# A four-layer linear-attention encoder stage: its engine order written out by hand, its attention placed between the other half's feed products

## The chip, the cores and the metric

The kernel runs on one core of a Trainium2 chip. The metric is device microseconds of one execution of the whole kernel, in which the stage spoken of here is one of eleven.

## The reference, cut to what matters

The kernel computes a four-layer network on 16 sequences of 64 tokens with 256 features (1024 tokens). The second stage of layer 0, `l0_attn` in the kernel, is an encoder of its own with four layers, all in float32:

```python
def _linear_attention(q, k, v):
    qp = jax.nn.elu(q) + 1.0
    kp = jax.nn.elu(k) + 1.0
    kv = jnp.einsum('bshd,bshm->bhmd', kp, v)
    ksum = jnp.sum(kp, axis=1)
    z = 1.0 / (jnp.einsum('blhd,bhd->blh', qp, ksum) + EPS_ATTN)
    return jnp.einsum('blhd,bhmd,blh->blhm', qp, kv, z)

def _encoder_layer(x, ...):
    h = _layernorm(x, ln1_s, ln1_b)
    q, k, v = h @ Wq + bq, h @ Wk + bk, h @ Wv + bv      # 16 heads of 16
    x = x + (_linear_attention(q, k, v) @ Wo + bo)
    h = _layernorm(x, ln2_s, ln2_b)
    return x + (relu(h @ W1 + b1) @ W2 + b2)             # 256 -> 1024 -> 256
```

The stage is `x = x + LN(encoder(sqrt(256) * LN(x) + pos))`: the encoder works on a copy `y`, and the last LayerNorm (`lnf_s`, `lnf_b`) is added to the residual x. A later stage, a cross attention over a context of 16 x 1601 rows, needs the sum of squares of each context row; these sums have nothing to do with the encoder, but they are taken during this stage, 208 instructions of 128 rows each.

## The kernel before

The 1024 tokens are eight tiles of 128, in two halves of four tiles, `a` and `b` (class `Half`). Each half goes through three steps per layer:

- `project`: `norm` (statistics, a square root on ScalarE, the normalisation), transposes to feature-major `hT`, the queries `qT` by feature (`by_feature`, 512 columns a product), keys `kz` and values `va` by token (`by_token`), then `elu1` (lines 338 to 340) over the whole half: a minimum with 0 on GpSimd, Exp on ScalarE, and a combination on VectorE, once for the queries and once for the keys.
- `attend`: per tile of 128 tokens (two sequences j) the key-value sums `pk` (`sums`, line 493: 64 rows of the array), masked on VectorE to `kv`; then `apply` (line 504: 64 columns of the array) to `po`; division on VectorE, transposes, the output product with `wo` and its addition to `y` (line 526).
- `feed`: `norm` and transposes again, W1 by feature with ReLU (`bias_relu`, lines 345 and 347, alternating VectorE and ScalarE), W2 by token.

`add_row` (line 429) adds an output bias to the whole half of `y` on GpSimd. `squares(n)` draws the next n of the context's sums of squares (`context_squares`, lines 2059 to 2070) and is called after each product; their input comes in 32 pieces over SyncE's DMA queue, and with this calling pattern all 208 are done in the first 150 us of the stage.

The order of the work is the scheduler's. The program text gives priorities (for each layer: project a, feed b of the layer before, attend a, project b, feed a, attend b), and the scheduler places every instruction on its engine by its own estimate of when its inputs are there. An engine works off its queue strictly in that order. Other stages of the kernel have their TensorE instructions in written order instead: with `self.pinned` set, `mm` and `tr` call `keep_in_program_order` on each instruction. [...]the stage uses two each for `mm`, `tr`, `kv` and `po`.

## Time and profile before

| | |
|---|---|
| median of three runs | 3892.77 us (3888.97 to 3895.52) |
| the profiled execution's own time | 3895.43 us |
| its span, first to last instruction | 3893.4 us |
| granted TensorE clock, mean | 0.958 of full |
| the stage: last product of the stage before ends, last `x` of this one is written | 864.8 to 1363.6 us |
| busy in 860 to 1365: TensorE, VectorE, ScalarE, GpSimd | 438.3, 257.9, 162.1, 101.5 us |

The profile is that of one execution. A row of the timeline has the start in us, the length in us, the engine, the line of the kernel, the operation, output<-input, its shape and how many are merged in the row; in brackets is how long the engine stood idle before it and what released it. PE is TensorE (PEld its weight loads), DVE VectorE, ACT ScalarE, POOL GpSimd, SPq the queue of SyncE that issues DMAs. A float32 product appears as two MATMUL records. In the table of windows each row is one stretch of time: its bounds, its length, then the busy time of each engine with the number of its instructions in brackets, the granted TensorE clock (1.00 is full), the DMA share and GB/s. A period of the steady state, one half through one layer, takes 58.4 us: the same transposes begin at 1146.2, 1204.6 and 1263 us.

### The profile page before, as it was taken

How to read it: one execution, taken by the hardware profiler on the slowest of the kernel's cores; microseconds unless marked ns; L12 is line 12 of the kernel's file. 1: busy time of each engine (PE TensorE's matmuls, PEld its weight loads, DVE VectorE, ACT ScalarE, POOL GpSimd, SP SyncE). 2: the span in 40 equal slices, each digit the busy share in tenths (PEclk: the TensorE clock that was granted, in tenths of full speed). 3: DMA queues.
4: the chain of work that ended last, by engine and by line, in shares of the span. 5: the costliest groups of instructions: out<-in, count | busy, mean ns of one | idle time of the engine just before them, and what ended most of it. 6: DMA issues, size and time to landing. Idle time of an engine off the chain costs nothing.

```text
span 3893.4 us, 71039 instructions
## 1 busy us (share of the span) xinstructions
PE 3559.3 (91%) x31163; PEld 2254.0 (58%) x31178; DVE 2001.7 (51%) x3655; ACT 1415.8 (36%) x1987; POOL 1311.5 (34%) x756
## 2 busy tenths in 40 slices
PE   8999999988989889999987898899999889999985
PEld 4555555555556555555545666567777656555554
DVE  4334333345454445655656554567676656333346
ACT  2333333346411111444433433266666612111223
POOL 1555555552221101433431100377777630000011
PEclk9999999999999989999998999999999979999987
DMA  3111111015200005222401000311111004111640
GB/s 122 37 37 37 37 37 37 19 52 204 101 33 25 22 22 176 106 77 100 141 26 38 1 6 1 104 40 54 37 55 37 2 10 167 39 35 32 286 156 13
DMA packets 97373, 248.84 MB, mean 64 GB/s; under 512 B 7924, under 2 KB 68991, under 8 KB 94888
## 3 DMA queue, kind: packets, MB, share of 16 engines
q1 hardware_dynamic: 97064, 244.31, 17.7%
q8 instruction: 244, 4.00, 0.4%
q14 instruction: 65, 0.53, 0.0%
HBM read 243.24 MB, written 1.05 MB: 63 GB/s over the span
## 4 chain that ended last, share of the span: by engine, by line
PE 55%; DVE 10%; ACT 3%; issue 2%; POOL 1%; DMA 1%; DVEq 0%; ACTq 0%; SPq 0%; POOLq 0%
PE pk L2050 9%; PE sc L2050 7%; PE lin L179 5%; PE pu L2050 3%; PE acc L2050 3%; PE gate L1622 3%; PE up L1622 3%; PE pc L1249 3%; PE prz L2050 2%; PE lin_t L166 2%; PE lin L445 2%; PE turn L2055 1%; PE gelu_t L1159 1%; PE lin_t L435 1%; PE lin L2050 1%
## 5 line engine op out<-in xcount | busy, mean ns | idle before, releaser
L1986 POOL TENSOR_TENSOR tot<-tot,e 128x1024 f32<-128x1024 f32 (+1 forms) x340 | 803.0, 2362 | 375.0 <-ACT e L307 252.2
L250 DVE TENSOR_REDUCE m<-sc 128x4 f32<-128x2048 f32 x96 | 220.1, 2293 | 273.3 <-PE sc L2050 272.2
L1389 DVE SCALAR_TENSOR_TENSOR e<-sc,row_L_xattn_nbias,free 128x2048 f32<-128x2048 f32 x104 | 244.3, 2349 | 124.5 <-PE sc L2050 118.9
L1391 ACT ACTIVATE e<-e 128x2048 f32<-128x2048 f32 x104 | 198.7, 1910 | 243.3 <-DVE e L1389 243.3
L2050 PE MATMUL sc<-qb,kT 32*128 32x128 f32 x6656 | 247.2, 285 | 39.6 <-DVE m L264 12.3
L307 ACT ACTIVATE e<-sc 128x2048 f32<-128x2048 f32 x104 | 195.2, 1877 | 241.5 <-PE sc L2050 236.5
L2050 PEld LDWEIGHTS sc<-qb,kT 32*128 32x128 f32 x6656 | 208.2, 188 | 84.8 <-issue 25.1
L2050 PE MATMUL acc<-e,v 128*32 128x128 f32 x6656 | 228.4, 278 | 6.7 <-ACT e L1392 6.6
L2050 PEld LDWEIGHTS acc<-e,v 128*32 128x32 f32 x6656 | 171.4, 110 | 105.4 <-issue 95.0
L2050 PE MATMUL pk<-cT,wk 128*128 128x512 f32 (+1 forms) x512 | 207.6, 534 | 3.6 <-DVE rows L280 3.6
L2050 PE MATMUL pk<-wv,cT 128*128 128x256 f32 x832 | 208.6, 393 | 0.0
L1392 ACT ACTIVATE e<-e 128x2048 f32<-128x2048 f32 x104 | 198.7, 1911 | 3.3
L2050 PE MATMUL pk<-cT,wkv 128*128 128x512 f32 (+1 forms) x512 | 196.5, 524 | 0.0
L2050 PE MATMUL pk<-wkv,cT 128*128 128x256 f32 x832 | 196.3, 386 | 0.0
L2050 PEld LDWEIGHTS pk<-wv,cT 128*128 128x128 f32 x832 | 149.2, 189 | 75.3 <-issue 57.2
L2050 PEld LDWEIGHTS pk<-wkv,cT 128*128 128x128 f32 x832 | 153.2, 190 | 28.4 <-issue 4.3
L1249 PE MATMUL pc<-ew,eh 128*128 128x256 f32 x640 | 159.0, 392 | 0.0
L794 POOL TENSOR_TENSOR e<-e,mx 128x512 f32<-128x512 f32 x96 | 81.6, 882 | 211.9 <-DVE mx L793 211.9
L2050 PE MATMUL sc<-kT,qb 32*128 32x512 f32 (+2 forms) x1536 | 140.3, 462 | 13.0 <-issue 1.5
L2050 PE MATMUL pu<-cn,e 128*64 128x257 f32 (+1 forms) x1248 | 143.9, 387 | 5.6 <-POOL e L804 5.6
L1626 ACT ACTIVATE g<-gate 128x512 f32<-128x512 f32 x68 | 40.6, 597 | 293.3 <-PE gate L1622 293.3
L2050 PE MATMUL sc<-cT,qT 128*64 128x512 f32 (+1 forms) x768 | 142.3, 519 | 1.0 <-DVE qT L752 0.5
(484 smaller groups left out, 6434.2 us busy)
## 6 DMA issues: line engine op xcount, KB each, us to landing
cT<-in_ctx_t SPq DMA_DIRECT2D x128, 832.0 KB
cn<-in_ctx_n SPq DMA_DIRECT2D x32, 1664.0 KB
piece<-in_ctx_n SPq DMA_DIRECT2D x16, 896.0 KB
piece<-in_ctx_n SPq DMA_DIRECT2D x16, 768.0 KB
w<-in_L_attn_W SPq DMA_DIRECT2D x8, 1024.0 KB
w<-in_L_ffn_W SPq DMA_DIRECT2D x16, 256.0 KB
down<-in_L_ffn_w_down SPq DMA_DIRECT2D x16, 256.0 KB
gate<-in_L_ffn_w_gate SPq DMA_DIRECT2D x16, 256.0 KB
```

The costliest lines, as they stand in the source:

```text
L166: nc.tensor.matmul(pm, w[:, k, n * P : (n + 1) * P], xT[:, k, h * 512 : (h + 1) * 512], start=(k == 0), stop=(k == kc - 1),)
L179: nc.tensor.matmul(pm, xT[:, k, t * P : (t + 1) * P], w[:, k, :], start=(k == 0), stop=(k == kc - 1))
L250: nc.vector.tensor_reduce(x.m4[:, g, :, i], pm, AX.X, ALU.max)
L307: nc.scalar.activation(e, pm, AF.Exp, scale=0.25)
L794: pin(nc.gpsimd.tensor_tensor(p.e, p.e, p.mx.unsqueeze(2).to_broadcast(p.shape), ALU.subtract))
L1249: nc.tensor.matmul(pc[:, n, j, :], s.eh[i][:, c, tok], ew2[:, c, cols], start=False, stop=(c == 3))
L1389: nc.vector.scalar_tensor_tensor(e16, pm16, nb, free[:, at : at + P].unsqueeze(1).to_broadcast([P, 16, P]), ALU.add, ALU.mult)
L1391: nc.scalar.activation(e, e, AF.Relu)
L1392: nc.scalar.activation(e, e, AF.Square)
L1622: nc.tensor.matmul(pm[-1], w[:, k, n * P : (n + 1) * P], xT[:, k, tok], start=(k == 0), stop=(k == KC - 1))
L1986: nc.gpsimd.tensor_tensor(tot[:w], x.first if c == 1 else tot[:w], e[:w], ALU.add)
L2050: ins = self.nc.tensor.matmul(*args, **kw)
```

## The change

`Written` wraps an engine so that each of its instructions is kept in program order. In `l0_attn` all of VectorE's, ScalarE's and GpSimd's instructions go through it (`V`, `A`, `G`), and TensorE's through `mm` and `tr` with `pinned` set. The steps become generators that stop after each piece, and hand-written loops step them: `project` of one half alongside the transposes of the other half's `feed`, then `mix`, which puts one or more pieces of `attend` of one half behind each product of `feed` of the other half.

The operations change too:

- `norm` is split into `measure` (statistics and square root) and `norm` (reciprocal and normalisation), each for a pair of tiles.
- The transposed tile's first half of features is taken out by VectorE, the second by ScalarE (before: both by VectorE); in `attend` ScalarE takes both at once.
- elu + 1 is computed as max(min(exp(z), 1), z + 1): the bias is raised by 1 beforehand (`bq1`, `bk1`, on GpSimd), ScalarE takes the exponential of the queries straight out of PSUM and of the keys from `kz` with bias -1, and one VectorE instruction per 512 columns combines them. GpSimd's minimum is gone.
- In `sums` the two sequences alternate, and each has a PSUM bank of its own. The banks are now three for `mm`, two for `tr`, two for one `kv`, one for `po`.
- The 208 squares are spread evenly, 26 to each `feed`, and their input comes in 48 smaller pieces, three ahead, whose DMAs are issued by ScalarE.
- The start (`begin`) and the last LayerNorm (`finish`) are done by pairs of tiles; the row `lnf` is loaded at the start.

```diff
+class Written:
+
+
+    def __init__(self, tc, engine):
+        self.tc, self.engine = tc, engine
+
+    def __getattr__(self, name):
+        def issue(*args, **kw):
+            self.tc.keep_in_program_order(getattr(self.engine, name)(*args, **kw))
+        return issue
...
+            ps = ctx.enter_context(tc.tile_pool(name="l0a_ps", bufs=1, space=PSUM))
+            V, A, G = (Written(tc, e) for e in (nc.vector, nc.scalar, nc.gpsimd))
+            pieces = self.context_squares(sb2, A)
...
+            def measure(s, src, p):
+
+                mv = sb2.tile([P, 2, 2], F32, tag=f"ln_mv{s.i}", name="ln_mv")
+                for j in range(2):
                     st = sb2.tile([P, 6], F32, tag="ln_st", name="ln_st", bufs=3)
+                    V.bn_stats(st, src[:, 2 * p + j, :])
+                    V.bn_aggr(mv[:, j, :], st)
+                r = sb2.tile([P, 2], F32, tag=f"ln_r{s.i}", name="ln_r")
+                V.tensor_scalar(r, mv[:, :, 1], 1.0, 1e-5, ALU.mult, ALU.add)
+                A.activation(r, r, AF.Sqrt)
+                s.by[p] = mv, r
+
+            def norm(s, src, p):
+
+                mv, r = s.by[p]
+                V.reciprocal(r, r)
+                for j in range(2):
+                    t = 2 * p + j
+                    V.tensor_scalar(s.n[:, t, :], src[:, t, :], mv[:, j, 0:1], r[:, j : j + 1], ALU.subtract, ALU.mult)
+
+            def turn(s, p, scale=None, shift=None):
+
+                pt = ps.tile([P, KC, 2, P], F32, tag="tr", name="tr", bufs=2)
+                for c in range(KC):
+                    for j in range(2):
+                        self.tr(pt[:, c, j, :], s.n[:, 2 * p + j, c * P : (c + 1) * P], self.ident)
+                tok = slice(2 * p * P, (2 * p + 2) * P)
+                if scale is None:
+                    A.copy(s.hT[:, :, tok], pt.rearrange("p c j x -> p c (j x)"))
+                    return
+                of = [pt[:, c].rearrange("p j x -> p (j x)") for c in range(KC)]
+                V.tensor_scalar(s.hT[:, 0, tok], of[0], scale[:, 0:1], shift[:, 0:1], ALU.mult, ALU.add)
+                A.activation(s.hT[:, 1, tok], of[1], AF.Identity, bias=shift[:, 1:2], scale=scale[:, 1:2])
...
+                w.bq1 = sb2.tile([P, KC], F32, tag="bq1", name="bq1")
+                w.bk1 = sb2.tile([P, D], F32, tag="bk1", name="bk1")
+                for out, of in ((w.bq1, w.bq), (w.bk1, w.bk)):
+                    G.tensor_scalar(out, of, 1.0, 0.0, ALU.add, ALU.add)
...
+                def kv(t):
+                    pm = by_token(w.wkv, t, s.hT)
+                    V.tensor_tensor(s.kz[:, t, :], pm[:, 0:D], w.bk1, ALU.add)
+                    V.tensor_tensor(
+                        s.va[:, t, :, 0:128], pm[:, D : 2 * D].rearrange("p (g x) -> p g x", g=2),
+                        w.bv.rearrange("p (g x) -> p g x", g=2), ALU.add)
+
+                def two(t):
+                    return (a[:, t : t + 2, :].rearrange("p t x -> p (t x)") for a in (s.kz, s.tmp))
+
+                def exp_keys(t):
+                    z, e = two(t)
+                    A.activation(e, z, AF.Exp, bias=less)
+
+                def larger(z, e):
+                    V.scalar_tensor_tensor(z, e, 1.0, z, ALU.min, ALU.max)
+
+                qe = [s.h1T[:, c, :] for c in range(KC)]
+                turn(s, 0, w.ln1_s, w.ln1_b)
+                yield
+                for t in range(2):
+                    kv(t)
+                    yield
+                turn(s, 1, w.ln1_s, w.ln1_b)
                 add_row(s, w.bo)
+                exp_keys(0)
+                yield
+                for c in range(KC):
+                    pm = by_feature(w.wq, c, s.hT)
+                    A.activation(qe[c], pm, AF.Exp, bias=w.bq[:, c : c + 1])
+                    A.activation(s.qT[:, c, :], pm, AF.Identity, bias=w.bq1[:, c : c + 1])
+                    larger(*(two(0) if c == 0 else (s.qT[:, 0, :], qe[0])))
+                    yield
+                kv(2)
+                larger(s.qT[:, 1, :], qe[1])
+                yield
+                kv(3)
+                yield
+                exp_keys(2)
+                larger(*two(2))
...
+                    pk = ps.tile([P, 2, 512], F32, tag="kv", name="pk")
                     for g in range(2):
                         for j in range(2):
+                            o = slice(j * S, (j + 1) * S)
+                            self.mm(
+                                pk[:, j, g * 136 : (g + 1) * 136], s.kz[o, t, g * P : (g + 1) * P], s.va[o, t, g, :],
+                                start=True, stop=True)
+                    kv = sb2.tile([P, 2, 2, 136], F32, tag="kv", name="kv")
+                    for j in range(2):
+                        V.tensor_tensor(
+                            kv[:, j], pk[:, j, :272].rearrange("p (g x) -> p g x", g=2),
+                            mask.unsqueeze(1).to_broadcast([P, 2, 136]), ALU.mult)
+                    kvs[t] = kv
...
+                    sums(t)
+                    yield
+                    if t:
+                        apply(t - 1)
+                        yield
+                apply(HT - 1)
+                turn(s, 0)
+                yield
+                turn(s, 1)
+                yield
+                for t in range(HT):
+                    pm = by_token(w.wo, t, s.hT)
+                    V.tensor_tensor(s.y[:, t, :], pm, s.y[:, t, :], ALU.add)
+                    if t % 2:
+                        measure(s, s.y, t // 2)
+                    yield
+                    if t % 2:
+                        norm(s, s.y, t // 2)
+                        yield
+
+            def feed(s, w, last=False):
+
+                for p in range(2):
+                    turn(s, p, w.ln2_s, w.ln2_b)
+                    if p:
+                        add_row(s, w.b2)
+                    yield
+                for c in range(8):
+                    pm = by_feature(w.w1, c, s.hT)
+                    to, b1 = s.h1T[:, c, :], w.b1[:, c : c + 1]
+                    if c % 2:
+                        V.tensor_scalar(to, pm, b1, 0.0, ALU.add, ALU.max)
+                    else:
+                        A.activation(to, pm, AF.Relu, bias=b1)
+                    squares(1 + c % 2)
+                    yield
+                for t in range(HT):
+                    pm = by_token(w.w2, t, s.h1T)
+                    squares((4, 4, 4, 2)[t])
+                    V.tensor_tensor(s.y[:, t, :], pm, s.y[:, t, :], ALU.add)
+                    if t % 2:
+                        measure(s, s.y, t // 2)
+                    elif t:
+                        finish(s, 0, last)
+                    yield
+                finish(s, 1, last)
...
+            def finish(s, p, last):
+                norm(s, s.y, p)
+                if last:
+                    o = slice(2 * p, 2 * p + 2)
+                    sc = lnf[:, :D].unsqueeze(1).to_broadcast([P, 2, D])
+                    V.tensor_tensor(s.n[:, o], s.n[:, o], sc, ALU.mult)
+                    V.tensor_tensor(s.x[:, o], s.x[:, o], s.n[:, o], ALU.add)
...
+            def begin(s):
+
+                measure(s, s.x, 0)
+                yield
+                measure(s, s.x, 1)
+                yield
+                for p in range(2):
+                    mv, r = s.by[p]
+                    less = sb2.tile([P, 2], F32, tag=f"less{s.i}", name="less")
+                    V.tensor_scalar(less, mv[:, :, 0], -1.0, 0.0, ALU.mult, ALU.add)
+                    V.reciprocal(r, r)
+                    V.tensor_scalar(r, r, math.sqrt(D), 0.0, ALU.mult, ALU.add)
+                    for j in range(2):
+                        t = 2 * p + j
+                        A.activation(s.n[:, t, :], s.x[:, t, :], AF.Identity, bias=less[:, j : j + 1])
+                        V.scalar_tensor_tensor(s.y[:, t, :], s.n[:, t, :], r[:, j : j + 1], pos, ALU.mult, ALU.add)
+                    measure(s, s.y, p)
+                    yield
+                    norm(s, s.y, p)
+                    yield
+                G.tensor_tensor(s.x, s.x, lnf[:, D:].unsqueeze(1).to_broadcast([P, HT, D]), ALU.add)
...
+            def mix(at, fd):
+
+                for f, t in ((2, 1), (1, 1), (1, 2), (1, 2), (1, 1), (1, 1), (1, 1), (1, 2), (1, 3), (1, 1), (1, 0)):
+                    go(fd, f)
+                    go(at, t)
...
+            self.pinned = True
             a, b = Half(0), Half(1)
             w = weights(0)
             for s in (a, b):
                 nc.gpsimd.memset(s.va[:, :, :, 128:136], 1.0)
+            st = begin(a)
+            go(st, 4)
+            pr, st2 = project(a, w), begin(b)
+            go(pr, 1)
+            go(st)
+            for n in (1, 1, 1, 2, 1, 99):
+                go(pr, n)
+                go(st2, 1)
+            go(st2)
+            at, pr = attend(a, w), project(b, w)
+            go(pr, 4)
+            for _ in range(4):
+                go(at, 2)
+                go(pr, 1)
+            go(pr)
+            go(at)
+            at, fd = attend(b, w), feed(a, w)
+            go(fd, 2)
+            mix(at, fd)
             for l in range(1, 4):
                 w0, w = w, weights(l)
+                for s, ws, o, wo in ((a, w, b, w0), (b, w, a, w)):
+                    fd2, pr = feed(o, wo, l == 3 and o is a), project(s, ws)
+                    go(pr, 1)
+                    go(fd2, 1)
+                    go(fd)
+                    go(pr, 3)
+                    go(fd2, 1)
+                    go(pr)
+                    at, fd = attend(s, ws), fd2
+                    mix(at, fd)
+            go(fd)
+            go(feed(b, w, True))
+            squares(999)
+            self.pinned = False
...
+    def context_squares(self, pool, act):
+
+        todo = [(b, lo, min(lo + 5, NCH)) for b in range(B) for lo in range(0, NCH, 5)]
+        loaded = []
+        for i, (b, lo, hi) in enumerate(todo):
+            while len(loaded) < min(i + 3, len(todo)):
+                b2, lo2, hi2 = todo[len(loaded)]
+                piece = pool.tile([P, 5, D], F32, tag="piece", name="piece", bufs=3)
+                rows = self.d["ctx_n"][b2].rearrange("p (c x) -> p c x", x=D)
+                act.dma_start(piece[:, : hi2 - lo2, :], rows[:, lo2:hi2, :])
+                loaded.append(piece)
+            for c in range(lo, hi):
+                junk = pool.tile([P, D], BF16, tag="junk", name="junk")
+                act.activation(
+                    junk, loaded[i][:, c - lo, :], AF.Square, accum_out=self.ss[:, b // 2, c, b % 2 : b % 2 + 1])
+                yield
```

## The prediction

> **What bounds the kernel now.** I read the page first: TensorE is busy for 91% of the span and the chain that ended last is 55% TensorE, so a stage is worth what TensorE waits in it. Then the table of windows, asked for this stage's start, one steady period, its tail, and a stretch of another stage whose TensorE order is already written out:
>
> ```profile
> core 0: us, PE busy (x) PEld busy (x) DVE busy (x) ACT busy (x) POOL busy (x), PEclk, DMA share, GB/s
> 855.00:888.00 33.00, 22.37 (x138) 13.62 (x131) 25.91 (x77) 16.32 (x62) 13.05 (x7) 0.79 0.68 235
> 888.00:936.00 48.00, 36.52 (x199) 22.56 (x198) 28.85 (x78) 32.00 (x137) 14.20 (x5) 0.93 0.48 162
> ...
> 1146.20:1204.60 58.40, 52.29 (x225) 33.32 (x224) 28.94 (x81) 9.96 (x14) 11.93 (x4) 1.00 0.05 14
> ...
> 1321.50:1365.00 43.50, 32.17 (x108) 20.60 (x106) 19.25 (x50) 3.16 (x6) 2.35 (x1) 0.89 0.08 24
> ...
> 1600.00:1700.00 100.00, 99.30 (x629) 57.43 (x631) 66.82 (x183) 45.42 (x86) 42.88 (x53) 1.00 0.39 137
> ```
>
> In the steady period TensorE is idle for 58.40 - 52.29 = 6.1 us, at the start and the tail for 10 or 11 us each, part of that at a lowered clock (0.79, 0.89). The last row shows that a written order can hold TensorE at 99% with VectorE at 67%. Next the timeline of one steady period, for what ended each wait:
>
> ```profile
> 1148.34 3.70 PE L435 MATMUL lin_t<-hT,wq 128*128 128x512 f32 x8 [1.10 <-DVE hT L154]
> ...
> 1160.88 3.63 POOL L338 TENSOR_SCALAR tmp<-kz 128x1024 f32<-128x1024 f32 x1 [3.50 <-DVE kz L474]
> ...
> 1162.46 3.70 PE L435 MATMUL lin_t<-hT,w 128*128 128x512 f32 x8 [2.69 <-DVE hT L154]
> ...
> 1164.54 1.06 ACT L339 ACTIVATE tmp<-tmp 128x1024 f32<-128x1024 f32 x1 [6.07 <-POOL tmp L338]
> ...
> 1165.63 1.22 DVE L340 SCALAR_TENSOR_TENSOR kz<-kz,tmp 128x1024 f32<-128x1024 f32 x1 [2.77 <-ACT tmp L339]
> ...
> 1166.77 0.74 DVE L345 TENSOR_SCALAR h1T<-lin_t,vecs 128x512 f32<-128x512 f32 x1
> ...
> 1167.57 2.84 PE L435 MATMUL lin_t<-hT,w 128*128 128x512 f32 x6 [1.40 <-DVE h1T L345]
> ```
>
> Three waits, 1.10 + 2.69 + 1.40 = 5.2 us. None is a shortage of VectorE (29 us busy of 58): it stands in its queue behind something late. The third is plain: the elu of the keys goes GpSimd 3.63, ScalarE 1.06, VectorE 1.22 us, the ReLU output stands behind it on VectorE, and TensorE has only two `mm` banks. The other 0.9 us lie in `attend`, where the rows show a second loss:
>
> ```profile
> 1191.88 0.74 PE L493 MATMUL pk<-va,kz 64*128 64x136 f32 x8
> ...
> 1196.72 1.38 PE L493 MATMUL pk<-va,kz 64*128 64x136 f32 x8
> 1198.03 0.68 PE L504 MATMUL po<-kv,qT 128*64 128x136 f32 x8
> ```
>
> The same eight records take 0.74 or 1.38 us, the first where the two halves of the array's rows alternate (8 weight loads in 0.54 us there, 1.18 in the other).
>
> **The change, part by part.**
>
> *A steady period.* Its TensorE work at this trace's rates (start to start): 24 transposes at 0.13 = 3.1; queries 8 x 0.43 = 3.4; keys and values 16 x 0.43 = 6.9; W1 32 x 0.43 = 13.7; sums 4 x 0.70 = 2.8; apply 4 x 0.65 = 2.6; W2, 64 in 13.81 us by the chain, 13.8; wo 16 x 0.216 = 3.5. Sum 49.8 us. Now I lay the new order out over it. In `mix` the products of the other half's feed (1.7 us each for W1, 3.45 for W2) cover every chain of `attend`: two `kv` masks 0.9 us, then r, reciprocal and division 0.8, transposes and copies 0.6; nothing is late. Two waits remain, at the seam. After the last W2 product VectorE must do y, two pairs of statistics and the variance (0.45 + 0.8 + 0.15 us) before it takes out `hT` for the next `project` (0.5), while TensorE has only 8 transposes (1.05 us): 1.0 us idle. Then the queries wait for the second `hT`, with 4 transposes as cover: 0.4. That makes 51.3; with 0.7 for changes of tiling and small slips, 52.0 us against 58.4. The other way round, 58.4 less 6.1 idle, less 1.3 for sums now alternating everywhere, plus the 1.4 of new waits, is 52.4. I take 52.0: 6.4 us in each of six periods, 38 us.
>
> *VectorE* in such a period, with the rates of this trace (statistics 0.39 a tile, y and kz and va 0.33, n 0.35, hT 0.48, ReLU 0.67): about 25 us; half of `hT` goes to ScalarE, two combinations of 1.22 us become four of half that. Covered by 52.
>
> *ScalarE*: hT 4 x 0.37, keys' and queries' Exp and the queries' Identity 6 x 0.69 (the 512-column row), ReLU 4 x 0.69, copies 2 x 0.59, square roots 4 x 0.2, 26 squares at 0.40 start to start = 10.4, two table loads, six DMA issues. An issue on ScalarE is not in this trace; SyncE's row for such a piece is 0.33 us. From below it is no gain, since ScalarE issued none; from above it is 3.7 us, the mean of SyncE's waits before those issues:
>
> ```profile
> SPq L2066 <- ACT junk L2069: 102.7, 28, 6.9
> ```
>
> Those waits are for ScalarE's own squares, which in ScalarE's queue are already done, so I take 0.33: 2 us per period, some 25.5 us in all. Even at 3.7 it would be 46, under 52. If the cover went, 20 us a period would be at stake. Nobody on TensorE waits for SyncE's queue in this stage, so freeing it of 32 issues is worth nothing.
>
> *GpSimd* loses 16 minima of 3.6 us and gains eight small bias additions (0.9 us each, by the length of 3.6 for 1024 columns); their rows land long before use, though the load of `lnf`, moved to the start, stands 0.33 us ahead of the first of them on SyncE's queue: nothing. Its `add_row` (2.35 us) stays, behind the normalisation as now.
>
> *Table loads.* The trace's row:
>
> ```profile
> 1152.84 1.28 ACT L339 ACT_TABLE_LOAD   x1
> ```
>
> The instruction before it ends at 1152.82, so it costs 1.28 us and nothing besides. Before there are 15; walking the written order, I count 19. The Trainium skill ("ScalarE: Activation LUTs", What ACT_TABLE_LOAD costs) adds a drain of about 1.38 us to each. In a steady period (2 loads) both fit in ScalarE's 26 spare us; by the one the stage's start (about four loads on the path) pays 5 us, by the other 10 or 11. I take the row.
>
> *Changes of tiling.* The Trainium skill ("TensorEngine Tiling (Array Packing)", Key Properties) says that a change of tiling mode drains TensorE. This speaks against threading `attend` between full-array products: 14 changes per period, by my count of the written order. But the timeline shows 11 before, and one costs little: the last W2 record starts at 1191.57, `pk` at 1191.88, 0.31 against a rhythm of 0.216. A full drain would be that record's length less the rhythm, 0.16. Three more changes are 0.3 us a period by the row, 0.5 by the drain.
>
> *The start.* Now the first transpose is at 873.66, 8.85 us after TensorE ran dry. By pairs of tiles the chain is statistics 1.7, root with load 1.5, shift and y 1.4, statistics and root 1.4, n 1.0: transposes near 868. Then the start is bound by VectorE and ScalarE in turn: project a is stretched by half b's `begin`, and the square roots between the Exps cost loads; b's first `hT` stands behind all of it, at about 894. With 21 us of TensorE work for attend a and project b, and 6 us in which the two normalisations of a are exposed, W1 of layer 0 starts at 922, against 936 before. But before, attend b was largely done by then; it now adds 9 us, the first pieces' landing 3, a cooled clock 3. The boundary to layer 1 comes at 966 instead of 971: 5 us.
>
> *The tail.* From the last steady boundary before (1321.5) to the last x (1363.6) is 42.1 us. Now: 4.6 until W1, 13.7 + 13.8 of products, and y, statistics, root, n and the last LayerNorm for two tiles, 3.9: 36 to 37. Gain 5 us.
>
> **Sum.** 38 + 5 + 5 = 48 us off the profiled execution's 3895.4 (span 3893.4), which is 2.7 over the median of the runs; off the median, 3845, and 3844 with the floor's extra room counted. Two runs of one kernel here differ by up to 0.17%; about 0.2% (8 us) is what can be told from no change.
>
> **Rivals.**
>
> *Half the gain* (chance 0.17). In-order queues on three engines make small waits that I laid out as covered: a copy behind squares, a relu behind a division. At 55 us a period: 3.4 x 6 = 20, plus 5 for start and tail, 3868. For it: in before's stage the waits were of this kind too. Against: the 99% of the written stage.
>
> *Slower: ScalarE becomes the bound* (0.05). If each of its six issues in a period blocks it for long, relus, copies and `hT` stand behind it. Without issues it has 23.5 us; it passes the old 58.4 only when an issue costs (58.4 - 23.5) / 6 = 5.8 us. At 7 us it gives 65.5 a period, 7 x 6 = 43 us slower, 3935. Against: only the longest of SyncE's waits reaches 6.9.
>
> *No difference* (0.03): the start is worse by 40 us because VectorE, ScalarE and cold TensorE run one after another. It would eat all that the periods bring, 3893. Before, the same steps took 71 us to 936; nothing in them doubles.
>
> **How the numbers follow.** The main case has 0.75: 3844. With periods of 51.0 to 53.5 us (29 to 44 us), a start from -2 to +10 and a tail of 2 to 7, it spans about 3832 to 3864. The range runs from 3830 to 3869 to take in half the gain. Faster by over 0.2%: 0.92; same 0.03; slower 0.05.
>
> **What would show it.** Right: a period of 51 to 53.5 us, `pk` always near 0.7 us per eight, no wait of TensorE over 1.5 us in a period, waits at the seam on `hT`; first transposes near 868; ScalarE near 45% busy. Wrong: TensorE waiting for ScalarE's `hT`, `qT` or `h1T` in `mix`, DMA issues on ScalarE of microseconds, a start later than 980, a granted clock under 0.95 in the steady periods.

## The result: 36.7 us faster, but a third of the predicted gain is missing from the stage

The changed kernel takes 3856.36 us (median of four runs, 3854.91 to 3857.84) against 3893.02 us (3888.97 to 3895.52) for the one before on the same chip: a ratio of 0.9903, 95% interval 0.9891 to 0.9916. I forecast 3844 us with a range of 3830 to 3869. The time lies in the range, the gain is 36.7 us where I had 48. The profiled execution has a span of 3856.1 us (before 3893.4).

First I measured the stage by itself, from the end of the last addition to `x` ahead of it to the last `x` it writes: 865.28 to 1363.61 = 498.3 us before, 865.30 to 1331.59 = 466.3 us after. That is 32.0 us. The other 5.3 us of the span's difference lie behind the stage (2529.8 us before, 2524.5 after). The edit does not reach there, and the cause stays open: lined up by instruction, the changed kernel first loses 1.6 us, then gains 3.9 near 760, 1.5 near 805 and 1.4 near 1100 us behind the stage, and other edited kernels part from before at other places. Every profile of an edited kernel below has 2517 to 2525 us for that part, so the stage's own length is the sharper yardstick, and I use it from here on.

The table of windows of the changed kernel: start, start of layer 0's first feed and attend, one steady period, tail. Columns are the bounds in us, the length, busy time per engine with the count of instructions, the granted TensorE clock, the DMA share and GB/s:

```profile
core 0: us, PE busy (x) PEld busy (x) DVE busy (x) ACT busy (x) POOL busy (x), PEclk, DMA share, GB/s
864.90:900.00 35.10, 16.69 (x36) 7.36 (x36) 25.75 (x80) 15.31 (x27) 8.88 (x8) 0.78 0.14 44
900.00:976.07 76.07, 64.73 (x309) 40.18 (x310) 39.31 (x118) 26.46 (x79) 5.94 (x4) 0.92 0.24 73
976.07:1028.58 52.51, 50.71 (x226) 31.68 (x225) 27.78 (x80) 23.94 (x74) 4.66 (x2) 1.00 0.27 84
1291.10:1331.60 40.50, 30.67 (x105) 19.64 (x103) 17.48 (x43) 15.21 (x61) 2.35 (x1) 0.92 0.24 80
```

The period fell from 58.4 to 52.5 us, and TensorE now works for 50.7 of it. But in the first 35 us TensorE is busy for less than half (16.7 us), at 0.78 of its clock.

The timeline of the changed kernel answers to the waits shown of before. The first row is the seam between two periods, the second the queries, the third the key-value sums, the fourth an issue of a DMA by ScalarE (ACTq is its queue):

```profile
1030.98 3.70 PE L2198 MATMUL lin<-wkv,hT 128*128 128x512 f32 x8 [1.37 <-DVE hT L58]
...
1035.98 1.55 PE L2198 MATMUL lin_t<-hT,wq 128*128 128x512 f32 x3 [0.43 <-DVE hT L58]
...
999.74 0.73 PE L2198 MATMUL pk<-va,kz 64*128 64x136 f32 x8
...
992.37 0.33 ACTq L58 DMA_DIRECT2D piece<-in_ctx_n  x1
```

Line 58 is the helper `Written`, so every pinned instruction of VectorE, ScalarE and GpSimd carries it. Of the waits of before only two are left, 1.37 + 0.43 us, both on `hT` at the seam, and a DMA issue on ScalarE costs 0.33 us as I had taken it.

### The profile page after: what moved, and what is told of

Read it like the earlier page. It is cut to its first block, busy times and chain, and to the rows that moved or that the text cites. A ratio compares the mean times of both kernels' runs of the same rounds, so it can differ in the third digit from the quotient of the medians.

```text
span 3856.1 us, 71175 instructions
## 1 busy us (share of the span) xinstructions
PE 3540.6 (92%) x31178; PEld 2237.7 (58%) x31178; DVE 1996.7 (52%) x3673; ACT 1455.9 (38%) x2067; POOL 1258.6 (33%) x749
## 4 chain that ended last, share of the span: by engine, by line
PE 77%; DVE 12%; ACT 7%; issue 2%; DMA 1%; POOL 0%; ACTq 0%; SPq 0%; DVEq 0%; POOLq 0%
PE sc L2198 15%; PE pk L2198 15%; PE lin L2198 6%; PE acc L2198 6%; PE lin L191 5%; PE lin_t L2198 5%; ACT e L319 5%; PE pu L2198 3%; PE gate L1770 3%; PE up L1770 3%; PE pc L1397 3%; PE prz L2198 2%; PE lin_t L178 2%; PE gelu_t L1307 2%; PE turn L2203 2%
```

## The experiments

Time is the median; the ratio is to the kernel before on the same chip. "Stage" is from the profile, as defined above; "to layer 1" runs from its beginning to the first key-value product of layer 1 (a wait is behind it); "period" is the distance of these products, as a mean (in before the first is 60.0 us, the other four 58.4 each).

| kernel | us | ratio [95%] | stage | to layer 1 | period |
|---|---|---|---|---|---|
| before | 3893 | 1 | 498.3 | 109.8 | 58.4 |
| changed | 3856.36 | 0.9903 [0.9891, 0.9916] | 466.3 | 113.2 | 52.5 |
| serial_sums | 3856.35 | 0.9913 [0.9896, 0.9929] | 466.5 | 113.3 | 52.5 |
| nosq | 3852.68 | 0.9896 [0.9878, 0.9913] | 466.3 | 113.2 | 52.5 |
| start | 3849.2 | 0.9893 [0.9878, 0.9908] | 459.4 | 106.2 | 52.5 |
| seam | 3843.34 | 0.9875 [0.9861, 0.989] | 452.8 | 112.1 | 51.3 |
| nomix | 3921.11 | 1.0077 [1.0054, 1.01] | 534.8 | 120.4 | 62.6 |
| free_all | 3818.41 | 0.9814 [0.98, 0.9829] | 431.3 | 90.0 | 51.3 |
| free_vec | 3825.76 | 0.9834 [0.9814, 0.9853] | 438.4 | 97.8 | 51.3 |
| free_nomix | 3845.29 | 0.9889 [0.9867, 0.9911] | 456.7 | 90.2 | 54.4 |
| free_old_elu | 3855.2 | 0.9907 [0.9886, 0.9927] | 467.9 | 95.0 | 56.5 |
| begin_free | 3822.97 | 0.9814 [0.9798, 0.9829] | 433.6 | 92.9 | 51.3 |
| free_best | 3818.69 | 0.9805 [0.9788, 0.9822] | 429.9 | 89.6 | 51.3 |
| free_best2 | 3814.57 | 0.9794 [0.9779, 0.981] | 431.5 | 91.2 | 51.3 |

(In the kernel before, the queries stand ahead of the key-value products, so its "to layer 1" ends 3.3 us later in a steady period than that of the changed kernel. Counted to the boundary itself, in before one steady period of 58.4 ahead of the transposes at 1029.35, it is 105.7 us there and 110.8 in the changed kernel. The first period of before is really 60.0 us; with that its boundary lies 1.6 us earlier, and the start of the changed kernel loses 6.7 us instead of 5.1.)

### Is it the written order? (free_all, free_vec)

My theory was that pinning all engines makes the gain. The test takes the pinning away and leaves everything else, text order included:

```diff
-            V, A, G = (Written(tc, e) for e in (nc.vector, nc.scalar, nc.gpsimd))
+            V, A, G = nc.vector, nc.scalar, nc.gpsimd
...
-            self.pinned = True
```

> All operations of the change, but neither TensorE nor the other engines are held in written order in this stage; the scheduler places them. If the written order makes the gain (my theory), the steady periods fall back towards 56 to 59 us and the time to 3880 to 3900. If the rival is right, that the new operations make it (elu without GpSimd, outputs shared with ScalarE, three banks, alternating sums), the periods stay below 54 us and the time below 3866.

Measured: 3818.41 us, 38 us faster than the changed kernel. The theory fell. The windows of free_all at the start, in a period and at the tail:

```profile
861.00:900.00 39.00, 29.31 (x109) 13.94 (x108) 31.69 (x98) 25.85 (x76) 12.03 (x10) 0.87 0.45 151
900.00:950.70 50.70, 49.47 (x241) 32.64 (x239) 28.54 (x93) 31.75 (x129) 5.81 (x3) 1.00 0.51 154
950.70:1002.03 51.33, 50.70 (x225) 31.67 (x224) 27.98 (x80) 32.79 (x118) 4.71 (x2) 1.00 0.48 150
1259.40:1293.20 33.80, 28.84 (x105) 18.94 (x103) 16.22 (x39) 4.38 (x9) 0.00 (x0) 0.99 0.07 24
```

The steady period has the same 50.70 us of TensorE work as with everything pinned, in 51.33 instead of 52.51 us. At the start TensorE does 29.3 us of work in 39 where the pinned order did 16.7 in 35. The tail is 33.8 instead of 40.5 us. Over the stage 35.0 us: 23 up to layer 1, 6 in five periods of 1.17, and 6 at the end.

free_vec leaves `self.pinned = True`, so that TensorE alone is in written order:

> TensorE alone stays in written order; VectorE, ScalarE and GpSimd are left to the scheduler. If what the written order costs is that on the three elementwise engines (statistics behind all six x additions, hT behind y and statistics at the seam), this comes to the 3818 us of the kernel with nothing pinned, 3815 to 3825. Rival: TensorE's written order costs it as much (its queue holds a transpose or a weight product that waits at the start and ahead of the tail), then it stays at 3845 to 3856.

Measured: 3825.76 us. Of the 35 us in the stage, 28 belong to the order written on VectorE, ScalarE and GpSimd, and 7 to TensorE's. All of the latter lie ahead of layer 1 (97.8 against 90.0 us).

### Where the written order loses: the start

The rows of the changed kernel's timeline that lead to the first product of half b. VectorE's last addition to `x` is at 864.88:

```profile
864.88 0.42 DVE L345 TENSOR_TENSOR x<-lin,x 128x256 f32<-128x256 f32 x1 [0.44 <-PE lin L191]
...
865.35 0.43 DVE L58 BATCH_NORM_STATS2 ln_st<-x 128x6 f32<-128x256 f32 x1
...
872.38 1.13 PE L2203 MATMUL tr<-cst,n 128*128 128x128 f32 x4 [7.53 <-DVE n L58]
...
894.21 0.60 PE L2203 MATMUL tr<-cst,n 128*128 128x128 f32 x4
...
895.83 3.06 DVE L58 SCALAR_TENSOR_TENSOR y<-n,ln_r,cst 128x256 f32<-128x256 f32 x2 [0.30 <-ACT n L58]
896.22 1.28 ACT L58 ACT_TABLE_LOAD   x1
896.28 2.34 POOL L58 TENSOR_TENSOR x<-x,row_L_attn_lnf_s 128x1024 f32<-128x1024 f32 x1 [14.40 <-ACT n L58]
...
902.49 0.69 DVE L58 SCALAR_TENSOR_TENSOR kz<-tmp,kz 128x512 f32<-128x512 f32 x1 [1.65 <-ACT tmp L58]
...
903.94 0.54 DVE L58 TENSOR_SCALAR hT<-tr,vecs 128x256 f32<-128x256 f32 x1
...
904.63 5.69 PE L2198 MATMUL lin<-wkv,hT 128*128 128x512 f32 x8 [9.81 <-DVE hT L58]
```

The first statistics stand behind every addition to `x`: the pinned ones come after the last of them, so the first transposes are at 872.4 instead of the 868 I had. Later the transposes of half b are done at 894.8, but the `hT` that takes them out starts at 903.94. Between them on VectorE stand `begin` for b (two `y` in 3.06 us), statistics, and a `kz` that waits for an exponential behind a table load. In free_all the same transposes run at 884.30 and their `hT` at 885.17.

The 3.06 us is an effect of its own: the pair took 0.88 us at 869.18. In the slow case GpSimd's addition to `x` started 0.45 us after the first of the pair, and the second one ended only after it. A `ln_r` of 128x2 took 1.11 us at 877.13 (0.17 elsewhere) while the same kind of addition ran from 875.57 to 878.21. The Trainium skill ("SBUF — State Buffer", Who interferes with whom) states that a VectorE instruction with two SBUF inputs is blocked by a GpSimd instruction that reads SBUF until that one ends; the two `y`, whose inputs `n` and `pos` both lie in SBUF, agree. `ln_r` has one such input, so this sentence does not cover it. Which of the two comes first matters: the pair at 875.12 took only 0.89 us, and there it was GpSimd's addition that took 2.64 instead of 2.34 us.

The kernel start leaves the statistics of x of half a to the scheduler, and puts GpSimd's additions to `x` behind the first `mix`:

```diff
-                measure(s, s.x, 0)
+                by = (nc.vector, nc.scalar) if s.i == 0 else (V, A)
+                measure(s, s.x, 0, *by)
...
-                G.tensor_tensor(s.x, s.x, lnf[:, D:]..., ALU.add)     # at the end of begin
...
             mix(at, fd)
+            for s in (a, b):
+                G.tensor_tensor(s.x, s.x, lnf[:, D:]..., ALU.add)
```

> As after, but the first statistics of half a are left to the scheduler and GpSimd's addition of the last LayerNorm's shift to x is moved behind the first mix. My theory: in after these statistics stood behind six additions to x of the stage before (first at 865.35 us), and GpSimd's addition held up VectorE's y (3.06 us for a pair instead of 0.88); the first transposes come 4 us earlier, W1 of layer 0 5 to 7 us earlier, the kernel 5 to 7 us faster than after. The rival: the start is bound by table loads and the chain between the engines, and less than 2 us of it reach W1.

Measured: 3849.2 us; the stage is 6.9 us shorter, all ahead of layer 1 (106.2 against 113.2), with the first transposes at 869.05, 3.2 us behind the last `x` instead of 7.1. So under a third of the 23 us between this start and that of free_all is these two things. The rest lies in how the steps are threaded, which no run takes apart further; the next one only shows that it lies ahead of the first feed.

The kernel begin_free lets the scheduler place everything up to the first feed, and pins what follows, with the edit of seam (next):

```diff
-            V, A, G = (Written(tc, e) for e in (nc.vector, nc.scalar, nc.gpsimd))
+            V, A, G = nc.vector, nc.scalar, nc.gpsimd
...
-            self.pinned = True
...
+            self.pinned = True
+            V, A, G = (Written(tc, e) for e in (nc.vector, nc.scalar, nc.gpsimd))
             go(fd, 2)
             mix(at, fd)
```

> The written order begins only with the first feed: all that stands ahead of it (both normalisations of x, project and attend of half a, project of half b) is left to the scheduler on all engines, and the rest is pinned, with the seam and the tail as in the kernel seam (3843 us). If the 38 us between the changed kernel and the one with nothing pinned are the start (22 us), the seams (7 to 8) and the tail (6.6), this kernel has them all: 3818 to 3825. Rival: a part of the gain comes from the freedom inside the periods (W1 products early, squares wherever ScalarE is idle); then it stays at 3826 to 3836.

Measured: 3822.97 us. Its stage is 19.2 us shorter than that of seam, and 2.3 longer than that of free_all. The periods are 51.3 us as there. So the steady part loses nothing by being written out once its seam is right; the start does. Table loads do not decide the start: from 855 to 950 us begin_free has seven of them like the changed kernel, and free_all five.

### The seam and the tail

In the changed kernel the last `y` of a feed, its statistics and the variance (1028.78 to 1030.39) stand on VectorE ahead of the `hT` that TensorE waits for. seam puts the statistics behind the next transposes, and in the last period the other half's transposes ahead of the last LayerNorm:

```diff
-                    if t % 2:
-                        measure(s, s.y, t // 2)
-                    elif t:
+                    if t == 1:
+                        measure(s, s.y, 0)
+                    elif t == 2:
                         finish(s, 0, last)
                     yield
+                measure(s, s.y, 1)
                 finish(s, 1, last)
...
+            fd2 = feed(b, w, True)
+            go(fd2, 2)
             go(fd)
-            go(feed(b, w, True))
+            go(fd2)
```

> As after, but the statistics of the feed's last pair of tiles are written behind the transposes' outputs of the next project and feed, and at the tail the other half's outputs come ahead of the last LayerNorm. My theory: the 1.37 us wait of TensorE at each seam is only VectorE's place in the queue; it falls below 0.5 us, the 5.4 us wait at the tail below 2: seven times 0.9 and 3.5, 8 to 10 us faster than after. The rival: the normalisation of the second pair, now later, takes the wait's place in front of the next transposes, and the period stays at 52.5 us within 0.4.

Measured: 3843.34 us. Timelines: the tail's first product in the changed kernel, then a seam and the tail in seam.

```profile
1297.58 15.79 PE L2198 MATMUL lin_t<-hT,w 128*128 128x512 f32 x32 [5.42 <-DVE hT L58]
```

```profile
1026.78 3.70 PE L2201 MATMUL lin<-wkv,hT 128*128 128x512 f32 x8 [0.20 <-DVE hT L58]
...
1283.91 14.00 PE L2201 MATMUL lin_t<-hT,w 128*128 128x512 f32 x32 [0.65 <-DVE hT L58]
```

The wait fell from 1.37 to 0.20 us at each seam (1.0 us ahead of layer 1, five periods of 1.17 = 5.9) and from 5.42 to 0.65 at the tail, whose 32 records then take 14.00 instead of 15.79 us (6.6 together). The stage is 13.5 us shorter. The theory of VectorE's queue held. The gain is above the 8 to 10 us expected, since the wait at the tail fell by 4.8 where I had 3.5, and since the low clock behind it went too (1.8 us).

### Interleaving, elu and pinning belong together (nomix, free_nomix, free_old_elu)

Whole feed ahead of whole attend, once with everything pinned (nomix) and once with nothing (free_nomix):

```diff
-                for f, t in ((2, 1), (1, 1), (1, 2), (1, 2), (1, 1), (1, 1), (1, 1), (1, 2), (1, 3), (1, 1), (1, 0)):
-                    go(fd, f)
-                    go(at, t)
+                go(fd, 12)
+                go(at)
```

> All engines stay in written order, as in the changed kernel, but feed of one half stands wholly ahead of attend of the other. Now nothing can fill attend's chain of sums, mask, apply, division, transposes, output product: four applies of about 0.65 us each wait for a mask of 0.9 us behind only one sums (0.7), and the last division, transposes and copy of about 2 us are bare, so some 4 to 6 us more per period in seven periods: 3885 to 3900. Rival: VectorE runs ahead far enough that only the end of attend is bare, 1 to 2 us per period: 3863 to 3872.

> No engine is kept in program order (as in free_all, 3818 us), and in addition mix() is undone: the whole feed of one half is written ahead of the whole attend of the other, nothing between the products. If the placing of attend between the feed products is what the scheduler makes good use of (the text order as priorities), the periods go back towards the 58 us of before and the time to about 3860 to 3885. Rival: the operations (statistics by pairs, hT shared by two engines, elu without GpSimd, three mm banks) make the gain, and a scheduler free on all engines fills attend's waits by itself: under 3830.

Measured: 3921.11 and 3845.29 us. Pinned, the interleaving is worth 65 us, more than I expected; free, 27, between my two expectations. Left free, the scheduler threads the output product and the next transposes among attend's applies by itself (periods of 54.4 us); pinned, they stand where they are written. Why nomix is so slow shows in its timeline and windows (1 us each):

```profile
986.39 5.40 PE L2197 MATMUL lin<-wkv,hT 128*128 128x512 f32 x8 [3.05 <-DVE hT L58]
...
1030.35 0.73 PE L2197 MATMUL pk<-va,kz 64*128 64x136 f32 x8 [1.91 <-DVE kv L58]
...
1032.06 1.20 PE L2197 MATMUL pk<-va,kz 64*128 64x136 f32 x8 [0.36 <-DVE r L58]
```

```profile
1030.00:1031.00 1.00, 0.65 (x8) 0.56 (x8) 0.20 (x1) 0.00 (x0) 0.00 (x0) 1.00 0.99 348
1031.00:1032.00 1.00, 0.70 (x10) 0.43 (x8) 0.87 (x3) 0.00 (x0) 0.00 (x0) 1.00 1.09 388
1032.00:1033.00 1.00, 0.94 (x8) 0.91 (x8) 0.68 (x2) 0.00 (x0) 0.00 (x0) 0.59 0.37 129
1033.00:1034.00 1.00, 1.00 (x11) 0.74 (x8) 0.70 (x2) 0.00 (x0) 0.00 (x0) 0.50 0.01 3
1034.00:1035.00 1.00, 1.00 (x10) 0.71 (x8) 0.61 (x4) 0.00 (x0) 0.00 (x0) 0.50 0.00 0
1035.00:1036.00 1.00, 1.00 (x14) 0.70 (x12) 0.71 (x3) 0.00 (x0) 0.00 (x0) 0.71 0.00 0
```

A period of it is as a mean 10.1 us longer than that of the changed kernel (62.6 against 52.5). The one from 986.39 to 1047.96 is 9.1 us longer. Its bracketed waits add up to 7.9 us (1.8 in the changed kernel), 6.1 more. The rest is the clock. After waits of 1.91 and 0.36 us it is at 0.50 for some 3.3 us: eight `pk` take 1.20 us instead of 0.73, and the next `po` and `pk` are slowed likewise, 1.5 us together. The key-value products behind the wait of 3.05 us take 5.40 instead of 3.70. My expectation counted waits and no clock, hence its miss.

free_old_elu has elu as before (minimum on GpSimd, Exp on ScalarE, combination on VectorE, whole halves at the end of `project`), with nothing pinned and the interleaving kept:

```diff
-                    A.activation(qe[c], pm, AF.Exp, bias=w.bq[:, c : c + 1])
-                    A.activation(s.qT[:, c, :], pm, AF.Identity, bias=w.bq1[:, c : c + 1])
-                    larger(*(two(0) if c == 0 else (s.qT[:, 0, :], qe[0])))
+                    A.activation(s.qT[:, c, :], pm, AF.Identity, bias=w.bq[:, c : c + 1])
...
-                exp_keys(2)
-                larger(*two(2))
+                for z in (s.qT.rearrange("p c x -> p (c x)"), s.kz.rearrange("p t x -> p (t x)")):
+                    self.elu1(z, t2, z)
```

> No engine is kept in program order, and elu is taken back to the form of before (minimum on GpSimd, Exp on ScalarE, combination on VectorE, over the whole half at the end of project, bias without the 1). Against free_all at 3818 us: my reading of the profile of before was that the wait of 1.40 us for a ReLU behind the keys' elu came from it, so at least 1.4 us in each of seven periods, and in the stage's start the chain of 3.6 + 1.1 + 1.2 us in part: 3828 to 3840. Rival: with attend between the feed products and three mm banks that chain is hidden, 3816 to 3824.

Measured: 3855.2 us, 37 us slower than free_all, far over both expectations. The chain in one of its periods:

```profile
1193.49 3.62 POOL L350 TENSOR_SCALAR tmp<-qT 128x1024 f32<-128x1024 f32 x1 [4.63 <-ACT qT L533]
...
1198.24 1.22 DVE L352 SCALAR_TENSOR_TENSOR qT<-qT,tmp 128x1024 f32<-128x1024 f32 x1 [1.33 <-ACT tmp L351]
1199.54 3.62 POOL L350 TENSOR_SCALAR tmp<-kz 128x1024 f32<-128x1024 f32 x1 [2.43 <-DVE qT L352]
...
1203.20 1.06 ACT L351 ACTIVATE tmp<-tmp 128x1024 f32<-128x1024 f32 x1 [4.42 <-POOL tmp L350]
...
1204.29 1.23 DVE L352 SCALAR_TENSOR_TENSOR kz<-kz,tmp 128x1024 f32<-128x1024 f32 x1 [3.95 <-ACT tmp L351]
1205.57 0.73 PE L2194 MATMUL pk<-va,kz 64*128 64x136 f32 x8 [3.45 <-DVE kz L352]
```

The keys' minimum waits for the queries' combination, since both use `tmp`, so `kz` is ready only 12 us after the queries' minimum began. In the order of before a whole feed stood between `project` and `attend` and hid that. With attend begun among the first W1 products, TensorE waits 3.45 us for `kz`, and behind that wait its clock falls to 0.50. Against free_all, undoing the interleaving alone costs 27 us and undoing elu alone 37, of 74 us in all, so the two don't simply add up. Both undone at once was not measured. Nor were GpSimd, the shared `tmp` and the work on whole halves taken apart, or the other new operations (the shared `hT`, statistics by pairs, three `mm` banks).

### Alternation of the sequences and the squares (serial_sums, nosq)

```diff
-                    for g in range(2):
-                        for j in range(2):
+                    for j in range(2):
+                        for g in range(2):
```

> As after, but in each sums the two products of one sequence come before those of the other, so the array's row halves no longer alternate. If the alternation is worth what the two lengths in the trace before say (1.38 against 0.74 us per eight records), each period grows by 4 x 0.64 = 2.6 us and the kernel by 8 x 2.6 = 20 us, to about 3877. The rival: the records overlap with the products around them anyway, and nothing changes within 3 us.

Measured: 3856.35 us, and the 32 rows of eight `pk` in its stage are all at 0.74 us, one of them:

```profile
1044.17 0.74 PE L2198 MATMUL pk<-va,kz 64*128 64x136 f32 x8
```

The order of the sequences is worth nothing. In the steady part of before 10 such rows took 0.74 us and 5 took 1.38. What makes those five slow is in the trace of before, around the row of 1.38 us at 1196.72 that the prediction shows:

```profile
1193.14 0.73 PE L493 MATMUL pk<-va,kz 64*128 64x136 f32 x4 [0.52 <-DVE kv L496]
...
1196.89 0.43 DVE L496 TENSOR_TENSOR kv<-pk,cst 128x272 f32<-128x272 f32 x1
...
1197.37 0.53 PEld L493 LDWEIGHTS pk<-va,kz 64*128 64x128 f32 x4
```

Four records, one sequence, take 0.73 us alone, as long as eight of both together: the two sequences run side by side when they can. At 1196.72 they can't. The second one needs the PSUM bank that VectorE's mask `kv` empties from 1196.89 to 1197.32, and its first weight load starts at 1197.37. So the 1.38 us hide a wait for VectorE inside a row that shows none. The changed kernel gives a tile's two sequences both banks at once, and they run together in either order. Its `pk` keep TensorE busy for 2.94 us a period, those of before for 4.32. (No run has the old banks in the new order, so the part of the banks alone is not shown.)

nosq drops the calls of `squares` and with them their DMAs:

> The changed kernel without the 208 sums of squares of the context and without their DMAs: this part of the computation is left out (the sums are filled with a constant on VectorE), all the rest is as written. It shows what ScalarE's 10.4 us of squares and six DMA issues cost a period. My prediction put them at nothing, covered by a ScalarE that is busy for 24 of 52 us: 3850 to 3858, the periods at 52.5. Rival: squares stand in ScalarE's queue ahead of the ReLU outputs and transposed tiles that TensorE waits for, in the first mix above all: 3835 to 3848.

Measured: 3852.68 us, which is within the scatter outside the stage: its stage is 466.33 us, that of the changed kernel 466.29. ScalarE's busy time in a period falls from 23.9 to 13.1 us without moving TensorE:

```profile
976.00:1028.50 52.50, 50.71 (x224) 31.68 (x224) 27.76 (x82) 13.10 (x22) 4.67 (x2) 1.00 0.07 21
```

The squares and their issues are covered, as costed.

### A faster kernel (free_best, free_best2)

free_best is free_all with the edit of seam; free_best2 also writes the exponentials of the first `project` behind both normalisations, and the first transposes of half b earlier:

```diff
-            pr, st2 = project(a, w), begin(b)
+            pr, st2 = project_first(a, w), begin(b)     # exp_keys and Exp of the queries at its end
```

> Nothing pinned (free_all, 3818 us), with the text of the kernel seam: statistics of the last pair behind the next turns, and the other half's turns ahead of the last LayerNorm. The scheduler had already put the transposes' outputs ahead of the statistics at the seams (wait of 0.20 us), so I expect no difference that can be told: 3812 to 3824. Rival: the text order is what the scheduler goes by when two instructions are ready at once, and half a us a period and part of the tail are left in it: 3806 to 3811.

> free_best, and in the first project of half a the three exponentials stand behind both halves' normalisation of x in the text, so that fewer square roots come between exponentials (fewer table loads at 1.28 us each on ScalarE's path in the start). If table loads bound the start in the kernel with nothing pinned, two to four fewer give 2.5 to 5 us: 3808 to 3816. Rival: the scheduler already groups them, or TensorE at 0.87 of its clock and VectorE (32 of the first 39 us busy) bound the start: as free_best within 3 us, or a few us slower since the text keeps half a's attend back.

Measured: 3818.69 and 3814.57 us. free_best equals free_all: the scheduler had already placed the seam that way. free_best2 is lowest, but its stage (431.5 us) is not shorter than that of free_best (429.9), it has the same five table loads from 855 to 950 us (the changed kernel has seven), and the intervals overlap. So the three are one result: about 75 us under the kernel before, some 40 under the changed one.

## Why the prediction was partly right

Its steps, in the order of its sum:

- **Periods: right.** Forecast 52.0 us, measured 52.51; TensorE's work 49.8 plus 0.7 forecast, 50.71 measured; six times 5.9 = 35.4 instead of 38 us. Forecast waits at the seam 1.0 and 0.4, measured 1.37 and 0.43. No other wait is in the period, and the three of before are gone. (What the three cost was not quite their sum: in two of the five steady periods of before the clock fell to 0.50 at the wait of 2.68 us, the wait of 1.40 vanished behind the slower products, and W1's 32 records took 15.7 us in all either way.) But the reason given was too narrow. The old elu was charged with one wait of 1.40 us; in the new order it costs 5.1 us a period (56.5 against 51.3 in free_old_elu). And "the written order can hold TensorE at 99%" was read as a merit of writing it out: the scheduler, given the same text as priorities, does 51.33.
- **Sums, 1.3 us a period: right in size, wrong in mechanism.** The busy time of `pk` fell by 1.4 us a period (4.32 to 2.94), but not by alternation, as serial_sums shows. The two lengths were misread: the longer row holds a wait of the second sequence for VectorE. That the size came out right is luck.
- **ScalarE: right.** Forecast 25.5 us a period, measured 23.94 (46% busy), a DMA issue 0.33 us, all of it covered (nosq). The rival of a ScalarE that becomes the bound is out.
- **VectorE: a little low.** Forecast 25, measured 27.8; in the periods it mattered only at the seam.
- **Start: the step that failed.** Forecast a gain of 5 us, measured a loss of 5 (110.8 against 105.7 us to the boundary). "Transposes near 868" came at 872.38: the chain of statistics was costed by its durations (7.0 us, measured 7.03 from 865.35), but its first instruction stands behind the last of the additions to `x`, not some 4 us earlier. Half b's "first `hT` behind all of it, at about 894" came at 903.94: I had not counted the `kz` that waits for an exponential, nor that VectorE is blocked while GpSimd adds to `x`. W1 of layer 0 started at 936.31, not 922. Leaving all of this to the scheduler gives 19 us back (begin_free against seam).
- **Tail: half of it missing.** Forecast a gain of 5 us, measured 1.6 (42.1 to 40.5). W1 had 4.6 us from the boundary; it started after 6.5. On VectorE the last LayerNorm of half a (two instructions of 0.69 us) and a `ln_r` of 1.07 us, stretched as above, stand ahead of `hT`. Then the first products ran at a low clock, 15.79 us for 32 records that take 13.90 elsewhere:

```profile
1297.50:1300.00 2.50, 2.42 (x3) 1.18 (x4) 0.02 (x1) 0.63 (x2) 0.00 (x0) 0.50 0.00 0
1300.00:1302.00 2.00, 2.00 (x4) 0.76 (x3) 0.00 (x0) 0.61 (x2) 0.00 (x0) 0.69 0.00 0
1302.00:1304.00 2.00, 2.00 (x6) 0.95 (x5) 0.75 (x1) 1.28 (x7) 0.00 (x0) 1.00 0.68 186
```

- **The whole.** 35.4 - 5.1 + 1.6 = 31.9 us in the stage. That the total gain is 36.7 and not 32 comes from the 5 us behind the stage, whose cause stays open. "Half the gain" named small waits in the periods; they took 2.6 us of the 16 that the stage fell short, and 13.5 lay at its two ends.

## What to carry to other kernels

Write the text in the order in which the work should go, make each operation short enough for that order, and then measure it both pinned and unpinned: here undoing the text order or the shorter elu each cost a third to a half of the gain, and pinning all engines gave half of it back (35 of 67 us in the stage), most of that through the three elementwise ones. If an order is pinned, walk every queue at the two ends of the stage, where nothing covers, and ask what stands on VectorE ahead of the one output TensorE waits for; inside the steady state statistics belong behind the next transposes' outputs. A long wait at a stage's end cost its length and some 2 us more, by the half clock behind it. And a row that merges several records can hide a wait between them: look at the weight loads and at what frees the bank.

## What the runs showed of the hardware

- *The clock behind a wait.* TensorE's wait of 1.37 us at a seam left the clock at 1.00. Waits of 5.42 and 9.81 us were followed by 0.50 for about 3.5 us, at a price of 1.9 and 2.0 us (15.79 for 13.90 as in nomix, and 5.69 for 3.70). The Trainium skill ("TensorE: Matmul & The Clock Gate", HAM oscillation) asks for no gap above about 3.4 us. Shorter ones were enough here: in nomix 1.91 and 0.36 us within four us, each of the seven times. But length alone does not decide it: in before a wait of 2.67 to 2.69 us comes in five steady periods, and left the clock at 1.00 in three of them and at 0.50 in two (at 1045.62 and 1279.30). What decides stays open.
- *VectorE beside GpSimd.* One addition of 2.3 us on GpSimd held VectorE instructions of 0.17 us for 0.68 to 1.11 us, and a pair of 0.88 us for 3.06 us. It struck `ln_r`, with one SBUF input and two columns, as well as `y`, with two inputs.
- *Table loads and changes of tiling.* The row was right on the load: in the changed kernel one starts at 867.15, takes 1.28 us, and the next instruction of ScalarE starts at 868.45, so the further 1.38 us do not show. The two prices for three more changes of tiling, 0.3 and 0.5 us a period, can't be told apart: TensorE's work is 0.9 us above the sum of 49.8, everything included.
- *ScalarE's evacuation.* `hT` of 256 columns takes ScalarE 0.56 us, where I had estimated 0.37; VectorE takes 0.54.
